# A 16-batch graph-attention kernel on one core: loads issued in half-size or quarter-size pieces, and batch 0's self features by seven block products

## The chip, the core and the metric

The kernel runs on one core of a Trainium2 chip. A core has five engines that run side by side, each with its own queue of instructions in program order: TensorE (PE, matrix products into PSUM), VectorE (DVE), ScalarE (ACT), GpSimd (POOL), and SyncE (SP), which here only issues transfers (DMAs). The metric is the device time of one launch in microseconds (us); the median of several runs is compared.

## The reference

For each of 16 batches there are N = 512 nodes with F = 512 features, one condition vector of 512, and an adjacency with 11 labels (here filled with zeros). The first NG = 20 nodes are the neighbours.

```
self_feat = concat(x, q or 0) @ W_self.T + b_self           # q only where a row of x sums to non-zero
output = self_feat
for d in 2 directions:
    kv = self_feat[:, :20];  qh = self_feat @ Wq[d].T + bq;  kh = kv @ Wk[d].T + bk     # 16 heads of 32
    aff = qh . kh / sqrt(32), masked where the labels' sum is 0, plus (labels @ w_bias + b_bias)
    output += (softmax(aff) @ kv) @ Wout[d] + bout
return x + relu(output)
```

## The kernel before

Everything is held transposed: features on the 128 partitions (four chunks c of 128), nodes in the free dimension. The kernel has a **setup** and a **loop** over batches b = 0 to 15, each with four tiles nt of 128 nodes.

**Setup** (lines 453 to 759). After the weights are loaded, `keys` (line 660) makes, in 22 bursts of eight matmuls, the keys already multiplied by Wq for all batches. A burst fills two PSUM buffers (`ps_g`), ACT empties one (line 684), DVE the other (line 686), into a staging tile `st`; from there SP stores them in DRAM, `g1_d` for batch 1 (line 694) and `g_d` for batches 2 to 15 (line 695). Both buffers are filled again by the next burst, so PE does other work between two bursts. The list `plan` (line 714) says which: `v` and `w` are parts of the value products (`values`, line 636, whose results POOL sends to DRAM as `vw_d`), `c` bias scores, `n` row flags, `b` biases, and `s` is a quarter of a block of batch 0's self features (`self_feat`, line 191, the plain product of x and W_self, finished by `self_copy`, line 210, on DVE). Three of the four blocks of batch 0 are made so in the setup; the fourth is made in the loop, in tile 1 of batch 0 (line 864).

**Self features of later batches** are made one batch ahead, in the loop, by seven products of half blocks instead of eight (a Winograd-Strassen scheme): `x_sum` (line 235) makes four sums of blocks of x on POOL, `weight_sums` (line 220) four of W_self once, `product` (line 246) runs the seven products in the order 1, 2, 6, 7, 5, 4, 3 into four PSUM banks (`ps_a` twice, `ps_d`, `ps_c`), and DVE adds them up in `partial` (line 281, on the accumulating `ps_a`) and `joined` (line 294). `partial` puts its first three results into tiles `u` of their own, from which `joined` reads.

**A tile of the loop**: `scores` (line 346, 128 matmul records in the profile) multiplies self features with the keys `gs[b]`; `weigh` (line 364, DVE) adds `full` (mask and bias, made by `full_add` on POOL, line 336), takes the maximum and subtracts it; `expo` is on ACT; `normal` (line 404) sums on DVE and multiplies on POOL; `turn` (line 410) transposes on DVE. In tile 2, `attend` (line 417) multiplies the previous batch's weights with its values `vds`, then come additions (`finish`), ReLU and the residual (POOL), and `store` (line 447).

**Order of the transfers.** All loads and stores of the loop are issued by SP in program order. `behind` (line 95) makes a load wait for a named instruction of another engine (`done["exp"]` and the like), so that the loads come at chosen places; whatever stands behind a waiting load on SP waits too. A batch loads x (1 MB, two loads), `adj` (twice 440 KB), `xn` (x in the other layout, for the row sums; twice 512 KB), the keys (twice 608 KB), `cq` (four of 20 KB), the row flags `nz` (256 KB, which `row_mask`, line 168, wrote to DRAM as `nz_d`, 2 KB, before) and the values `vd` (four of 32 KB, `load_values`, line 132), and stores four chunks of 256 KB.

**The start of the loop.** The keys of batch 1 are loaded ahead of the loop (line 770). In tile 1 of batch 0 SP issues the adjacency of batch 1, `cq`, one transfer of 2 MB that clears `bd_d` (`clear_blocks`, line 140), and the first `xn`. In tile 2 `blocks` (line 147) rearranges the values of all batches from `vw_d` into `bd_d`, by 12 transfers from DRAM to DRAM with rows of 128 bytes.

## Time and profile before

| what | value |
|---|---|
| median of 3 runs | 593.66 us (593.51 to 594.92) |
| the profiled execution: its own time | 593.27 us |
| the profiled execution: span from the first to the last instruction | 591.5 us (so 1.77 us lie around it) |
| TensorE clock granted, mean | 0.995 |
| PE busy | 578.7 us (98%) |
| DVE, ACT, POOL busy | 492.3, 395.6, 384.2 us |
| setup, up to the first scores | 92.5 us |
| one batch in the loop, the shortest | 30.47 us |

The page of the profile lists busy times, a picture of the span in 40 slices, the DMA queues, and the chain of work that ended last. A row of the chain has start, duration, engine, tile written, line and number of records. A row of the timeline has start, duration, engine, line, operation, tile written and tiles read; in brackets stands how long the engine was idle before it and what ended that. `issue` there means that the profile shows nothing that the engine waited for. PEld is TensorE's loading of weights. A product of the seven is 32 matmul records, and each matmul record has one record of a weight load.

### The profile page before, as it was taken

How to read it: one execution, taken by the hardware profiler on the slowest of the kernel's cores; microseconds unless marked ns; L12 is line 12 of the kernel's file. 1: busy time of each engine (PE TensorE's matmuls, PEld its weight loads, DVE VectorE, ACT ScalarE, POOL GpSimd, SP SyncE). 2: the span in 40 equal slices, each digit the busy share in tenths (PEclk: the TensorE clock that was granted, in tenths of full speed). 3: DMA queues.
4: the chain of work that ended last, by engine and by line, in shares of the span. 5: the costliest groups of instructions: out<-in, count | busy, mean ns of one | idle time of the engine just before them, and what ended most of it. 6: DMA issues, size and time to landing. Idle time of an engine off the chain costs nothing.

```text
span 591.5 us, 30038 instructions
## 1 busy us (share of the span) xinstructions
PE 578.7 (98%) x13180; PEld 439.7 (74%) x13180; DVE 492.3 (83%) x785; ACT 395.6 (67%) x1162; POOL 384.2 (65%) x351
## 2 busy tenths in 40 slices
PE   8999999999999999999999999999999999999994
PEld 6654547888978687787878787788787878787882
DVE  0495565889898888999999999888989898989896
ACT  1234644587877677768686868677787877777661
POOL 2315663638677675758686777675858677776774
PEclk9999999999999999999999999999999999999997
DMA  8998999857848485767676766757585748582503
GB/s 294 385 406 299 332 376 329 257 126 199 223 154 229 155 236 148 206 168 209 184 208 163 223 173 202 171 181 208 164 217 170 216 149 232 158 238 85 167 13 142
DMA packets 98129, 124.10 MB, mean 210 GB/s; under 512 B 19952, under 2 KB 70160, under 8 KB 95952
## 3 DMA queue, kind: packets, MB, share of 16 engines
q1 hardware_dynamic: 96752, 120.31, 67.1%
q8 instruction: 103, 1.69, 1.2%
q0 software_dynamic: 672, 1.36, 1.0%
q10 hardware_dynamic: 576, 0.53, 0.3%
q14 instruction: 26, 0.21, 0.1%
HBM read 82.30 MB, written 40.24 MB: 207 GB/s over the span
## 4 chain that ended last, share of the span: by engine, by line
PE 94%; DVE 3%; DMA 1%; issue 1%; ACT 0%; POOL 0%; SPq 0%; DVEq 0%; POOLq 0%; ACTq 0%
PE ps_s L353 44%; PE ps_a L279 17%; PE ps_c L279 8%; PE ps_o L426 6%; PE ps_d L279 4%; PE ps_v L644 3%; PE ps_k L581 3%; PE ps_sf L202 2%; DMA ws_q<-in_wsT 1%; PE ps_kv L532 1%; DVE o L435 0%; PE ps_nz L186 0%; DVE wt L415 0%; DVE ps_s L371 0%; DVE sm L406 0%
## 5 line engine op out<-in xcount | busy, mean ns | idle before, releaser
L353 PEld LDWEIGHTS ps_s<-g,sf 128*32 128x32 f32 x8192 | 264.0, 110 | 19.8 <-issue 12.2
L353 PE MATMUL ps_s<-g,sf 128*32 128x152 f32 x8192 | 277.3, 293 | 0.5 <-ACT st L684 0.5
L334 ACT COPY both<-add 32x80 f32<-32x80 f32 x512 | 130.9, 256 | 54.8 <-DVE add L325 49.0
L408 POOL TENSOR_TENSOR s<-s,sm 128x640 f32<-128x640 f32 x63 | 80.3, 1275 | 98.0 <-DVE sm L407 98.0
L341 POOL TENSOR_TENSOR full<-cq,both 128x640 f32<-128x640 f32 x64 | 100.1, 1565 | 30.3 <-issue 24.3
L314 ACT ACTIVATE prod<-adj,wb_sb 128x80 f32<-128x80 int32 x330 | 112.5, 432 | 0.0
L380 ACT ACTIVATE s<-s 128x640 f32<-128x640 f32 x63 | 46.5, 738 | 69.4 <-DVE s L375 69.0
L444 POOL TENSOR_TENSOR o<-o,x 128x512 f32<-128x512 f32 x60 | 75.9, 1285 | 0.0
L367 DVE TENSOR_TENSOR full<-ps_s,full 128x608 f32<-128x608 f32 x63 | 49.1, 779 | 32.1 <-PE ps_s L353 26.6
L406 DVE TENSOR_REDUCE sm<-s 128x32 f32<-128x640 f32 x63 | 50.9, 808 | 8.8 <-ACT s L380 8.6
L279 PE MATMUL ps_a<-t,ws_s 128*32 128x246 f32 x960 | 55.5, 370 | 0.0
L371 DVE TENSOR_REDUCE ps_s<-full 128x32 f32<-128x640 f32 x63 | 52.2, 828 | 2.2
L415 DVE STREAM_TRANSPOSE wt<-s 128x640 f32<-128x640 f32 x63 | 52.8, 839 | 0.1
L375 DVE TENSOR_TENSOR s<-full,ps_s 128x640 f32<-128x640 f32 x63 | 51.6, 818 | 1.1
L426 PE MATMUL ps_o<-wt,vd 32*32 32x512 f32 (+5 forms) x816 | 40.8, 581 | 3.7 <-DVE wt L400 2.0
L279 PEld LDWEIGHTS ps_a<-t,ws_s 128*32 128x32 f32 x960 | 32.2, 110 | 15.5
L325 DVE TENSOR_REDUCE add<-prod 128x80 f32<-128x960 f32 x32 | 36.8, 1150 | 6.3 <-ACT prod L314 4.4
L244 POOL TENSOR_TENSOR t<-x 128x492 f32<-128x492 f32 x30 | 34.4, 1148 | 10.1 <-DVE full L367 5.2
L439 ACT ACTIVATE o<-o,bo 128x512 f32<-128x512 f32 x60 | 38.2, 708 | 0.6 <-POOL biased L881 0.6
L435 DVE TENSOR_TENSOR o<-ps_o,sf 128x512 f32<-128x512 f32 x60 | 36.8, 672 | 1.0 <-PE ps_o L426 1.0
L286 DVE SCALAR_TENSOR_TENSOR u<-nz,qw,ps_a 128x246 f32<-128x246 f32 x90 | 36.6, 449 | 0.0
L244 POOL TENSOR_TENSOR t<-x,t 128x492 f32<-128x492 f32 x30 | 34.4, 1147 | 1.2
(238 smaller groups left out, 722.7 us busy)
## 6 DMA issues: line engine op xcount, KB each, us to landing
g_d<-st SPq DMA_DIRECT2D x16, 1064.0 KB, 5.9
g<-g_d SPq DMA_DIRECT2D x28, 608.0 KB, 5.2
out_T<-o SPq DMA_DIRECT2D x60, 256.0 KB, 4.7
xn<-in_xn SPq DMA_DIRECT2D x28, 512.0 KB, 3.6
x<-in_xT SPq DMA_DIRECT2D x28, 512.0 KB, 4.3
adj<-in_adj SPq DMA_DIRECT2D x32, 440.0 KB, 5.0
nz<-nz_d SPq DMA_DIRECT2D x14, 256.0 KB, 4.0
wk<-in_wkT SPq DMA_DIRECT2D x2, 1024.0 KB, 8.0
```

The lines of the kernel that those rows point to most:

```text
L244: nc.gpsimd.tensor_sub(t, one, two)
L279: nc.tensor.matmul(to, lhs, x[:, k], start=start, stop=stop, skip_group_check=n != 2)
L314: nc.scalar.activation(p[:, :, l], a[:, :, l], AF.Identity, scale=wb_sb[:, l : l + 1])
L334: nc.scalar.copy(adds[b, h][bass.ts(a, R), :, g], add[r].rearrange("p (t m) -> p t m", t=2))
L341: nc.gpsimd.tensor_add(f, cqs[b].unsqueeze(1).to_broadcast(shape), adds[b, nt // 2][:, nt % 2].unsqueeze(2).to_broadcast(shape),)
L353: nc.tensor.matmul(bank[bass.ts(a, R), bass.ts(j, WD // HL)], sfs[b][:, k, bass.ds(nt * P + (2 * g + j) * R, R)], keys[:, k, a], start=(k ...
L371: nc.vector.tensor_reduce(mx, f, AX.X, ALU.max)
L375: nc.vector.tensor_sub(s, f, mx.unsqueeze(3).to_broadcast(full))
L408: done["normal"] = nc.gpsimd.tensor_mul(s, s, sm.unsqueeze(3).to_broadcast(full))
L415: nc.vector.transpose(wts[b][:, nt], s.rearrange("p a h m -> p (a h m)"))
L426: nc.tensor.matmul(banks[a][bass.ds(at // 2 * DH, n * DH)].rearrange("p (t n) -> p t n", n=32), vd[r, bass.ds(at * DH, n * DH)], wt[r, :, ...
L444: nc.gpsimd.tensor_add(o[:, c], o[:, c], xs[b][:, c])
```

## The change

It has two parts.

1. **Batch 0's self features** are made wholly in the setup, by the seven products (step `p` in `plan`), each followed at once by its `partial` or `joined`. The values, flags and bias scores move to earlier bursts; the seven products are the fillers of the last seven bursts that have one. `row_sums(1)` and `weight_sums` move from bursts 11 and 13 to burst 9, and four `x_sum` for batch 0 are added on POOL in burst 11. The fourth block in tile 1 of batch 0 goes. `partial` now always writes into the self features' own tile, where `joined` adds to it (the tiles `u` go), and `new_self` (ACT) is called ahead of the first `partial`.
2. **The loop's loads** are split: x into four pieces of 256 KB, `xn` and the keys into four of 256 and 304 KB, `adj` into four of 220 KB, each behind an instruction of its own, in the order in which these come. Two pieces of x move ahead into tile 3 of the batch before. Each stored chunk is issued as soon as its residual is added. `load_values(b - 1)` moves from tile 3 of batch b - 1 to tile 0 of batch b. In batch 0 the clearing of `bd_d` becomes four transfers of 512 KB, `xn` four pieces, and `blocks` comes later, in tile 2 behind a sum; the second adjacency half of batch 1 and the keys of batch 1 are issued behind `blocks`.

On **PE**, in the setup, around the bursts of fc = 2, hg = 2 and 3 (a row is: line, operation, tile written, tiles read, size, how many alike). Before:

```order
L644 MATMUL ps_v_650<-wo_sb,kvT 128x512 x2
L669 MATMUL ps_g(2, 2, 1, 0, 2)0_688<-khD,wq_sb 128x304 x2
L669 MATMUL ps_g(2, 2, 1, 0, 2)1_689<-khD,wq_sb 128x304 x2
L202 MATMUL ps_sf_10_706<-x_161,ws_v 32x236 x16
L669 MATMUL ps_g(2, 3, 0, 1, 2)0_727<-khD,wq_sb 128x152 x2
L669 MATMUL ps_g(2, 3, 0, 1, 2)1_728<-khD,wq_sb 128x152 x2
L202 MATMUL ps_sf_10_706<-x_161,ws_v 32x236 x16
```

And in the changed kernel, at the same bursts:

```order
L189 MATMUL ps_nz<-rx_553,ones 128x512
L644 MATMUL ps_g(2, 2, 1, 0, 2)0_678<-khD,wq_sb 128x304 x2
L644 MATMUL ps_g(2, 2, 1, 0, 2)1_679<-khD,wq_sb 128x304 x2
L259 MATMUL ps_a_0_696<-x_161,ws_v 32x246 x8
L259 MATMUL ps_a_1_697<-x_161,ws_v 32x246 x8
L644 MATMUL ps_g(2, 3, 0, 1, 2)0_720<-khD,wq_sb 128x152 x2
L644 MATMUL ps_g(2, 3, 0, 1, 2)1_721<-khD,wq_sb 128x152 x2
L259 MATMUL ps_d_737<-x_161,ws_v 32x246 x16
```

Half a plain block (16 matmuls) between two bursts has become a whole product of the seven (16 matmuls too); the value products that stood around it are earlier.

On **SP**, from the last store of the setup to the first loads for batch 2 (`g_943` and `g_1193` are the keys of batch 1, `adj_1` the second half of its adjacency). Before:

```order
L695 DMA g_d<-st_885 128x2128
L130 DMA g_943<-g_d 128x16x152
L114 DMA adj_0_1038<-in_adj 128x2x440
L119 DMA cq_1040<-cq_d 32x160 x4
L142 DMA bd_d<-zero 128x16x256
L114 DMA adj_1_1046<-in_adj 128x2x440
L109 DMA xn_0_1048<-in_xn 128x1024
L109 DMA xn_1_1050<-in_xn 128x1024
L159 DMA bd_d<-vw_d 64x20x32
```

Changed, down to the first transfer of `blocks`:

```order
L670 DMA g_d<-st_913 128x2128
L117 DMA adj_0_1063<-in_adj 128x2x440
L145 DMA bd_d<-zero 128x4x256 x2
L122 DMA cq_1067<-cq_d 32x160 x4
L145 DMA bd_d<-zero 128x4x256 x2
L111 DMA xn_0_1152<-in_xn 128x512 x2
L111 DMA xn_1_1159<-in_xn 128x512 x2
L162 DMA bd_d<-vw_d 64x20x32
```

Changed, from the last two transfers of `blocks` on:

```order
L162 DMA bd_d<-vw_d 64x12x32
L162 DMA bd_d<-vw_d 64x20x32
L117 DMA adj_1_1191<-in_adj 128x2x440
L133 DMA g_1193<-g_d 128x4x152 x4
L105 DMA x_1467<-in_xT 128x512 x4
```

The keys of batch 1 have moved from the head of this piece to behind all twelve transfers of `blocks`, and so has the second half of its adjacency.

On **SP**, in batch 1, from the loads of x to the first keys. Before:

```order
L105 DMA x_1548<-in_xT 128x2x512 x2
L171 DMA nz_d<-nz_2_1583 128x4
L114 DMA adj_0_1609<-in_adj 128x2x440
L175 DMA nz_1639<-nz_d 128x512
L119 DMA cq_1641<-cq_d 32x160 x4
L114 DMA adj_1_1650<-in_adj 128x2x440
L109 DMA xn_0_1779<-in_xn 128x1024
L109 DMA xn_1_1781<-in_xn 128x1024
L130 DMA g_1895<-g_d 128x8x152
```

Changed:

```order
L105 DMA x_1467<-in_xT 128x512 x4
L174 DMA nz_d<-nz_2_1577 128x4
L139 DMA vd_1600<-bd_d 32x256 x4
L117 DMA adj_0_1608<-in_adj 128x440 x2
L178 DMA nz_1639<-nz_d 128x512
L122 DMA cq_1641<-cq_d 32x160 x4
L117 DMA adj_1_1650<-in_adj 128x440 x2
L111 DMA xn_0_1728<-in_xn 128x512 x2
L111 DMA xn_1_1783<-in_xn 128x512 x2
L133 DMA g_1790<-g_d 128x4x152 x2
```

Each load is split into two (x into four), and the values `vd` now stand between the write of the flags and the adjacency.

The diff, cut to its core (in the order of the code):

```diff
-    def load_xn(b, h, ins=None):
-        t = xns[b, h] = load.tile([P, 2, F], F32, tag="xn", name=f"xn{b}_{h}")
-        behind(nc.sync.dma_start(t, xn[b].rearrange("(p j) f -> p j f", j=4)[:, 2 * h : 2 * h + 2]), ins)
-
-    def load_adj(b, h, ins=None):
-        t = adjs[b, h] = load.tile([P, 2, S * L], I32, tag="adj", name=f"adj{b}_{h}", bufs=3)
+    def load_xn(b, h, ins=None, js=slice(0, 2)):
+        if js.start == 0:
+            xns[b, h] = load.tile([P, 2, F], F32, tag="xn", name=f"xn{b}_{h}")
+        rows = xn[b].rearrange("(p h j) f -> p h j f", h=2, j=2)[:, h]
+        behind(nc.sync.dma_start(xns[b, h][:, js], rows[:, js]), ins)
...
-    def clear_blocks(zero):
-
-        nc.sync.dma_start(
-            bd_d.rearrange("c b r e i g -> (c b r) (e i g)").rearrange("(n p) w -> p n w", p=P),
-            zero.unsqueeze(1).to_broadcast([P, C * B * 32 // P, HL * 2 * DH]),
-        )
+            ), ins if c == 0 else None)
+
+    def clear_blocks(zero, c, ins):
+
+        behind(nc.sync.dma_start(
+            bd_d[c].rearrange("b r e i g -> (b r) (e i g)").rearrange("(n p) w -> p n w", p=P),
+            zero.unsqueeze(1).to_broadcast([P, B * 32 // P, HL * 2 * DH]),
+        ), ins)
...
     def x_sum(b, n):
 
-        t = sums[b, n] = xsum.tile([P, 2, HN], F32, tag=f"t{n}", name=f"t{b}_{n}")
+        if b > 0:
+            t = xsum.tile([P, 2, HN], F32, tag=f"t{n}", name=f"t{b}_{n}")
+        else:
+            if n == 1:
+                held[0] = sfp.tile([P, C, N], F32, tag="sf", name="t0")
+            t = held[0][:, n - 1, : 2 * HN].rearrange("p (k n) -> p k n", k=2)
+        sums[b, n] = t
         one, two = {
             1: lambda: (x_block(b, 0, 1), x_block(b, 0, 0)),
             2: lambda: (x_block(b, 1, 1), sums[b, 1]),
             3: lambda: (x_block(b, 1, 1), x_block(b, 0, 1)),
             4: lambda: (x_block(b, 1, 0), sums[b, 2]),
         }[n]()
-        nc.gpsimd.tensor_sub(t, one, two)
+        done["xsum"] = nc.gpsimd.tensor_sub(t, one, two)
...
-    def partial(b, n, f, l, to=None):
-
-        if to is None:
-            to = us[b, n] = xsum.tile([P, 2, HN], F32, tag=f"u{n}", name=f"u{b}_{n}")
+    def partial(b, f, l):
+
+        to = block(b, f, l)
...
-    def joined(b, n, key, f, l):
-
-        nc.vector.tensor_add(
-            block(b, f, l), parts[b, key][:, : 2 * HN].rearrange("p (i n) -> p i n", i=2), us.pop((b, n))
+    def joined(b, key, f, l):
+
+        done["joined"] = nc.vector.tensor_add(
+            block(b, f, l), parts[b, key][:, : 2 * HN].rearrange("p (i n) -> p i n", i=2), block(b, f, l)
...
-            def self_step(b, f, h, i, k):
-                self_feat(b, f, h, ((i, (k,)),))
-                if (i, k) == (1, C - 1):
-                    self_copy(b, f, h)
+            def block_product(n):
+
+                product(0, n)
+                f, args = {
+                    1: (partial, (0, 0, 0)), 2: (joined, (0, "d", 0, 0)), 6: (partial, (0, 0, 1)),
+                    7: (partial, (0, 1, 1)), 5: (joined, (0, "c", 1, 1)), 4: (partial, (0, 1, 0)),
+                    3: (joined, (0, "c", 0, 1)),
+                }[n]
+                f(*args)
...
+                "p": [(block_product, (n,)) for n in (1, 2, 6, 7, 5, 4, 3)],
                 "v": [(values, (t, (d,), k)) for t in range(2) for d in range(2) for k in range(C)],
                 "w": [(values, (2, (0, 1), k)) for k in range(C)],
             }
-            plan = "bvv vv vv ccw vv ns ssss sssw vv vv ssss ssss vv vv nww ssss ssss".split()
+            plan = "bvv vvc vvc vvn vv vvw vv vv ww wn p p p p p p p".split()
...
+                if n == 9:
+                    row_sums(1)
+                    weight_sums()
                 if n == 11:
-                    row_sums(1)
-                if n == 13:
-                    weight_sums()
+                    new_self(0)
+                    for i in range(1, 5):
+                        x_sum(0, i)
...
-        load_keys(1)
...
-                    load_adj(1, 1)
-                    load_xn(2, 0)
-                    load_xn(2, 1)
-                if b == 0 and nt == 2:
-                    blocks()
-                if nt == 2 and last or nt == 3 and b == 0:
+                if nt == 2 and last:
...
-                            load_x(b + 1, range(2), done["exp"])
-                            load_x(b + 1, range(2, C), done["partial"])
+                            load_x(b + 1, range(2, 3), done["sum"])
+                            load_x(b + 1, range(3, C), done["normal"])
                         for g in range(2):
                             scores(b, nt, g, ps[g], range(2, C))
                         if more:
                             row_mask(b + 1)
                         mask_count(b, 1)
-                        joined(b, 3, "c", 1, 1)
+                        joined(b, "c", 1, 1)
                         product(b, 3)
+                        load_values(b - 1, done["joined"])
                         mask_sum(b, 1)
                         if more:
-                            load_adj(b + 1, 0, done["masks"])
+                            load_adj(b + 1, 0, done["masks"], slice(0, 1))
                     mask_spread(b, 1, (0, 1))
                     if last:
                         biased = work.tile([P, C, N], F32, tag="o", name="biased")
@@ -847,25 +822,26 @@
                     full_add(b, 1)
                     if more:
                         x_sum(b + 1, 1)
+                        if b > 0:
+                            load_adj(b + 1, 0, done["xsum"], slice(1, 2))
...
-                        load_nz(b + 1, done["exp"])
-                        load_cq(b + 1)
+                        load_nz(b + 1, done["weigh"])
+                        load_cq(b + 1, done["exp"])
                     normal(*prev)
+                    if b == 0:
+                        clear_blocks(zero, 2, done["sum"])
+                        clear_blocks(zero, 3, done["normal"])
                     if b > 0 and more:
-                        load_adj(b + 1, 1, done["normal"])
-                    if b == 0:
-                        self_feat(0, 1, 1)
+                        load_adj(b + 1, 1, done["normal"], slice(0, 1))
                     for g in range(2):
                         scores(b, nt, g, ps[g])
-                    if b == 0:
-                        self_copy(0, 1, 1)
...
+                            load_adj(b + 1, 1, done["xsum"], slice(1, 2))
+                        else:
+                            load_xn(2, 0, done["xsum"], slice(0, 1))
                         x_sum(b + 1, 3)
+                        if 0 < b < B - 2:
+                            load_xn(b + 2, 0, done["xsum"], slice(0, 1))
+                        elif b == 0:
+                            load_xn(2, 0, done["xsum"], slice(1, 2))
                     full_add(b, 2)
+                    if b == 0:
+                        load_xn(2, 1, done["full"], slice(0, 1))
...
-                            load_xn(b + 2, 0, done["add"])
-                            load_xn(b + 2, 1, done["relu"])
+                            load_xn(b + 2, 0, done["add", 1], slice(1, 2))
+                            load_xn(b + 2, 1, done["add", 3], slice(0, 1))
                     normal(*prev)
+                    if b + 2 < B:
+                        load_xn(b + 2, 1, done["sum"], slice(1, 2))
+                    if b == 0:
+                        blocks()
+                        load_adj(1, 1)
+                    if more:
+                        load_keys(b + 1, range(1), done["normal"])
                     for g in range(2):
                         scores(b, nt, g, ps[g])
                     if more:
                         product(b + 1, 1)
                         product(b + 1, 2)
-                    s = weigh(b, nt, pair, (lambda: partial(b + 1, 1, 0, 0)) if more else None)
+                        new_self(b + 1)
+                    s = weigh(b, nt, pair, (lambda: partial(b + 1, 0, 0)) if more else None)
                     expo(s)
                     turn(*prev)
-                    if b > 0 and more:
-                        load_keys(b + 1, range(2), done["exp"])
                     if more:
                         full_add(b, NT - 1)
+                        load_keys(b + 1, range(1, 2), done["full"])
                     if b > 0:
                         for c in (0, 1):
                             residual(b - 1, c, o)
+                            store()
...
+                    joined(b + 1, "d", 0, 0)
                     x_sum(b + 1, 4)
+                    load_keys(b + 1, range(2, 3), done["xsum"])
...
-                    partial(b + 1, 2, 0, 1)
+                    partial(b + 1, 0, 1)
                     mask_sum(b + 1, 0)
-                    if b > 0:
-                        load_keys(b + 1, range(2, C), done["masks"])
+                    load_keys(b + 1, range(3, C), done["normal"])
...
-                        residual(b - 1, 2, o)
-                        store()
-                        load_values(b)
-                        residual(b - 1, 3, o)
+                        for c in (2, 3):
+                            residual(b - 1, c, o)
+                            store()
+                    if b + 2 < B:
+                        load_x(b + 2, range(1), done["weigh"])
+                        load_x(b + 2, range(1, 2), done["exp"])
                     full_add(b + 1, 0)
```

80 lines of the change are left out of this document (25 added, 55 removed).

## The prediction

> **What bounds the kernel now.** I read the page first, then the windows of single stretches, then the chain of waits, and last the transfers around one stall. On the page I look at the busy times, the chain by engine and the queue of instructions.
>
> ```profile
> PE 578.7 (98%) x13180; PEld 439.7 (74%) x13180; DVE 492.3 (83%) x785; ACT 395.6 (67%) x1162; POOL 384.2 (65%) x351
> q8 instruction: 103, 1.69, 1.2%
> PE 94%; DVE 3%; DMA 1%; issue 1%; ACT 0%; POOL 0%; SPq 0%; DVEq 0%; POOLq 0%; ACTq 0%
> ```
>
> PE carries 94% of the chain, so only two things can pay: less work for PE, or fewer of the holes in it. The 1% "issue" is such a hole: PE waits for nothing that the program names. The 103 packets of queue 8 hold 1.69 MB, 16,384 bytes each. They are instructions: 13180 matmuls and as many weight loads, 26360 in all, are 256 to a packet.
>
> The windows give the span, then busy time and count of PE, PEld, DVE, ACT, POOL, then granted clock, DMA share and GB/s. The first is the end of the setup, the others are batches, from one tile 2 to the next; the last takes thirteen batches together.
>
> ```profile
> 59.00:92.00 33.00, 33.00 (x388) 16.40 (x384) 19.59 (x34) 16.16 (x39) 21.01 (x22) 1.00 0.96 354
> 135.77:166.72 30.95, 30.95 (x788) 26.61 (x792) 28.27 (x45) 23.67 (x71) 23.31 (x21) 1.00 0.76 205
> 166.72:198.55 31.83, 31.44 (x788) 24.27 (x792) 28.79 (x45) 24.29 (x73) 23.06 (x21) 1.00 0.66 194
> 198.55:230.66 32.11, 31.65 (x789) 24.46 (x792) 28.12 (x43) 23.75 (x73) 22.26 (x20) 1.00 0.65 184
> 261.14:291.62 30.48, 30.48 (x788) 24.15 (x792) 27.83 (x44) 23.53 (x71) 21.87 (x20) 1.00 0.67 191
> 352.77:384.77 32.00, 31.45 (x789) 24.34 (x792) 29.04 (x45) 24.48 (x73) 23.37 (x21) 1.00 0.69 190
> 384.77:415.92 31.15, 31.15 (x789) 24.32 (x792) 27.57 (x43) 22.65 (x71) 21.27 (x19) 1.00 0.67 190
> 135.77:538.00 402.23, 400.83 (x10196) 317.93 (x10200) 363.14 (x560) 305.87 (x923) 287.08 (x249) 1.00 0.68 191
> ```
>
> The setup has no hole in its last 33 us, at full clock. An undisturbed batch takes 30.48; thirteen of them would be 396.2, the loop takes 402.23, so **6.05 us** are lost. The five long rows have 0.47, 1.35, 1.63, 1.52 and 0.67 of it. The chain in the fourth of them shows the hole, in `attend`, and the page of transfers just ahead of it shows the load:
>
> ```profile
> 381.08 1.05 PE ps_o L426 x27
> 382.13 0.55 issue
> 382.68 2.10 PE ps_o L426 x21
> GB/s 239 223 398 334 445 382 368 398 121 66 48 33 58 96 27 55 14 27 41 14 0 0 14 14 14 0 123 123 123 55 41 123 123 178 287 396 424 383 287 232
> adj<-in_adj SPq DMA_DIRECT2D x1, 440.0 KB, 5.3
> q8 instruction: 1, 0.02, 5.2%
> ```
>
> The rate line covers 375.00 to 380.15 in 40 slices: after a rush the engines move mostly under 60 GB/s for about 2 us, then the 440 KB of `adj` rush through in some 1.2 us, and no packet of queue 8 is there. The one packet, last line, comes in the window 380.15 to 381.30, as the rush ends. PE runs dry about a microsecond later. So PE's next 256 instructions come late when their fetch falls behind a load's rush.
>
> **A, the setup.** The fourth block of batch 0 leaves the loop, and 3 blocks in the setup become seven products.
>
> ```profile
> 59.41 1.73 PE ps_sf L202 x32
> 86.82 1.86 PE ps_sf L202 x32
> 89.67 1.86 PE ps_sf L202 x32
> 96.86 3.45 PE ps_sf L202 x64
> 118.68 1.66 PE ps_a L279 x32
> ```
>
> Before there are six half blocks as fillers, four of 236 columns like the first row and two of 256 like the second and third: 4 x 1.73 + 2 x 1.86 = 10.64. A product of 246 columns took 1.66 in the loop. But 64 records of 256 columns took 3.45 there, 1.73 for 32, and 1.86 between bursts: being a filler costs 0.13. So a product as filler is 1.79 and seven are 12.5: **+1.9** (bounds: +1.0 at 1.66 each). I take 1.9, since the 1.86 row stands at the same place. The first scores move from 92.52 to 94.4.
>
> DVE has to empty a burst and sum a product in the time of one burst and one filler. The burst between the second and third row above lasts from 88.68 to 89.67, 0.99; with 1.79 that is 2.78:
>
> ```profile
> 86.91 1.17 DVE L686 TENSOR_SCALAR st<-ps_g(3, 2, 0, 1, 2)1_842 128x304 f32<-128x304 f32 x2 [0.34 <-PE ps_g(3, 2, 0, 1, 2)1_842 L669]
> 110.51 0.84 DVE L286 SCALAR_TENSOR_TENSOR u<-nz,qw,ps_a 128x246 f32<-128x246 f32 x2
> 103.01 1.14 POOL L244 TENSOR_TENSOR t<-x,t 128x492 f32<-128x492 f32 x1
> ```
>
> 1.17 + 0.84 = 2.01 against 2.78: hidden by PE's own work. POOL's four sums are 4.6 us, issued two bursts ahead of the products that need them, and POOL is busy for 21 of these 33 us: hidden. If that cover is gone, each late sum shows on PE one for one, at most about 1 us.
>
> **B and C, batch 0.** Here are PE's chain and the work on POOL and SP, where the clock of the batch starts at its first scores, T (92.52 before):
>
> ```profile
> 92.52 4.34 PE ps_s L353 x128
> 110.66 0.77 issue
> 123.67 4.13 PE ps_s L353 x128
> 105.31 1.56 POOL L341 TENSOR_TENSOR full<-cq,both 128x640 f32<-128x640 f32 x1
> 95.09 0.37 SPq L130 DMA_DIRECT2D g<-g_d  x1
> 104.61 1.96 SPq L109 DMA_DIRECT2D xn<-in_xn  x2
> 109.83 12.07 SPq L159 DMA_DIRECT2D bd_d<-vw_d  x12
> L159 SPq DMA_DIRECT2D bd_d<-vw_d x12: 611/716/1806, 109.8 to 121.2; - x12
> g<-g_d SPq DMA_DIRECT2D x28, 608.0 KB, 5.2
> ```
>
> The scores of batch 1 start at 123.67, T + 31.15. The block (3.45) goes, and with it perhaps the stall at 110.66 (some 0.98 with the slow start behind it): T + 26.7. DVE then comes to wait for POOL's `full` of tile 2, about 0.5: T + 27.2.
>
> But the keys of batch 1 are now **behind `blocks`** on SP. The last `xn` waits for `full` of tile 2, whose end is 105.31 + 1.56 = 106.87, T + 14.35; two issues bring `blocks` to T + 15.35, at 0.5 us each (one of the keys took 0.37, one `xn` of twice the size 0.98). Its twelve issues took 12.07, its median one 0.716, its shortest 0.611: 12 x 0.611 = 7.3 to 12.1. I take 12 x 0.86 = 10.3, the pace of the last seven:
>
> ```profile
> 115.89 6.01 SPq L159 DMA_DIRECT2D bd_d<-vw_d  x7
> g<-g_d SPq DMA_DIRECT2D x1, 1216.0 KB, 8.0
> DMA to landing us min/median/max: 3.4/4.4/4.9
> ```
>
> Then the second half of `adj` is issued (0.45, my estimate from the same two rows) and the keys, which land 5.2 us behind their issue by the median (8.0, the second row, while the engines were full; 3.4 at least, the landing of `blocks`' own, the third row). So the first quarter lands at T + 15.35 + 10.3 + 0.45 + 5.2 = T + 31.3; the next three are issued 0.45 apart and needed 1.03 apart. So PE, which could go on at T + 27.2, waits 4.1 us for the keys, and the block's gain is gone: **+0.15** (-3.95 at 7.3 and 3.4, where PE's floor holds; +4.7 at 12.07 and 8.0). With A that is **+2.05** up to the scores of batch 1 (-2.95 to +6.6). Queued behind this wait on PE is everything; on SP only loads of batch 2 stand behind, which have 20 us.
>
> **D, the loop.** PE, DVE, ACT and POOL do the same per batch. SP issues about 30 transfers instead of 20, each some 0.45 us: 14 of 30 us. Each load waits for an instruction that comes ahead of the next load's, so none holds up another for long, and I price the issuing at nothing; its cover is the 16 us in which SP has nothing to issue. What changes is the rush. Of `adj`, half stands behind the flags' write, 220 KB, and it waits for `masks`. If each stall shrinks by the 1.2 us of the rush, 0.47, 1.35, 1.63, 1.52 and 0.67 become 0, 0.15, 0.43, 0.32 and 0: 0.9. The fetches also slide (the setup's PE stream is shorter by 64 instructions), and may fall on other pieces: I add 0.6. So **1.5** of the 6.05 stay (bounds 0 and 5.55, since nothing in the trace shows the pieces): **-4.55**.
>
> [...]
>
> **Sum**, from the profiled execution's own 593.27: 593.27 + 1.9 + 0.15 - 6.05 + 1.5 = **590.8**. That execution is 0.39 under the median of 593.66, so my time may be as much low.
>
> **Rivals.**
>
> *The keys come in time and the holes close.* If `blocks` is issued at its shortest pace and the keys land fast, PE's floor counts: -3.95 + 1.9 = -2.05, and 5.55 of the loop's 6.05 go: 585.7. For it: `blocks` had the engines half idle at times in its 12 us; against it: only the minimum rows give it.
>
> *The change doesn't do what it says*: the holes don't come from the size of loads, but from the 2 us at under 60 GB/s behind the flags' small write, and that write stays. Then the loop gives 0.5 and the time is 593.27 + 2.05 - 0.5 = 594.8. For it: in the rate line the engines are slow long before the rush. [...]
>
> *Slower: the values come late.* `load_values` moves from tile 3 of a batch to tile 0 of the next, behind `joined`, two tiles ahead of `attend`:
>
> ```profile
> 281.83 0.66 DVE L296 TENSOR_TENSOR sf<-ps_c,u 128x492 f32<-128x492 f32 x1
> 289.38 2.24 PE L426 MATMUL ps_o<-wt,vd 32*32 32x512 f32 x48
> vd<-bd_d SPq DMA_DIRECT2D x64, 32.0 KB, 3.9
> ```
>
> `joined` ends at 282.49, four issues of some 0.4 us bring the last to 284.0, and `attend` starts at 289.38: 5.4 us are there, and the median landing is 3.9. From 5.4 on every tenth counts on PE, fourteen times. At 6.0 that is 0.6 x 14 = 8.4: 590.8 + 8.4 = 599.2. For it: the flags' write goes ahead; against it: 1.5 us of room.
>
> *Slow `blocks`*: +4.72 + 1.9 with 1.5 left in the loop: 593.27 + 6.62 - 4.55 = 595.3.
>
> **How the numbers follow.** Forecast 0.44 (its own range 588.4 to 592.8: nothing left in the loop and A at 1.0, or 3.5 left), keys in time 0.22, no effect 0.15, slow `blocks` 0.10, late values 0.09. The range from 585.5 to 595.5 holds all but the last and the tails. A measurement of this kernel can tell about 0.3%, 1.78 us, from no change: faster is under 591.88, slower over 595.44. Faster takes three quarters of the forecast and all of the first rival, 0.55; slower takes the late values and half of what ends near 595, 0.17; 0.28 are left for no difference.
>
> **What would show it.** First scores near 94.4, no `ps_sf` row, and seven `ps_a`, `ps_c`, `ps_d` rows near 1.79 in the setup: A. Scores of batch 1 at T + 31 with PE idle ahead of them and a DMA of `g` as releaser: C; no idle there: the first rival. Thirteen batches in 397.7 with rows of "issue" under 0.4 us: D; over 401: the second. Idle PE at `attend` released by `vd`: the third. The forecast is wrong most easily where the fetch falls on another transfer than I think, since its whole gain is in the holes.

## The result, and the profile after

The changed kernel took 594.46 us (median of 22 runs, 592.51 to 597.39), the kernel before 593.72 in the runs beside it (591.39 to 595.68). The ratio is **1.0008, interval 0.9994 to 1.0022**: no change that can be measured, where 590.8 was forecast. The profiled execution took 592.66 us, with a span of 590.8. It is 1.8 us under the median; what the median has beyond it no profile of these runs shows (e10 below, the same kernel on another chip, has a longer wait at the same place).

So a change that touches every load came out at nothing. The page shows where to look: PE has 4 us less to do (574.6 against 578.7), and yet PE's share of the chain is smaller.

```profile
PE 574.6 (97%) x13148; PEld 435.3 (74%) x13148; DVE 493.0 (83%) x788; ACT 395.0 (67%) x1162; POOL 388.6 (66%) x355
q8 instruction: 103, 1.69, 1.2%
PE 92%; DVE 4%; issue 1%; ACT 1%; DMA 1%; POOL 0%; DVEq 0%; POOLq 0%; ACTq 0%
```

Three windows cut the span at the same places in both kernels: from the fifth of the 22 bursts of `keys` (its second half; it is the first with a filler behind it) to the first scores (T), batch 0 up to the first scores behind its `attend`, and the thirteen batches after it. Before:

```profile
41.14:92.52 51.38, 50.85 (x532) 24.57 (x533) 31.07 (x58) 24.21 (x56) 29.73 (x34) 1.00 0.93 340
92.52:135.70 43.18, 42.41 (x1105) 35.83 (x1105) 33.26 (x51) 25.87 (x84) 20.78 (x21) 1.00 0.78 227
135.70:537.93 402.23, 400.83 (x10196) 317.94 (x10192) 363.14 (x560) 305.87 (x923) 287.08 (x249) 1.00 0.68 191
```

Changed:

```profile
40.35:92.70 52.35, 51.83 (x564) 24.95 (x564) 34.24 (x63) 24.21 (x56) 34.04 (x38) 1.00 0.93 335
92.70:140.84 48.14, 41.32 (x1041) 33.10 (x1041) 32.62 (x49) 25.91 (x84) 22.05 (x22) 0.96 0.80 219
140.84:537.14 396.30, 396.30 (x10196) 315.59 (x10192) 361.80 (x560) 305.26 (x923) 285.77 (x248) 1.00 0.67 193
```

The setup costs 0.97 more. The loop gives 5.93: its 396.30 us are those of thirteen undisturbed batches (396.2 by the prediction), so no hole is left in them. Lengths of batches tell this better than PE's idle time. Before, span less busy time is only 1.40 of the 6.05 us, since the ends of matmuls are modelled: in the hole that the prediction looked at, PE's row has 0.55 us of idle time and that of its weight loads 1.46, where the batch lost 1.52. Batch 0 takes all of it back: 48.14 against 43.18, although its PE executes 64 matmuls less. It is also the only stretch where the granted clock, third number from the right, is under 1.00. (0.97 + 4.96 - 5.93 is 0.00; the 0.6 us by which the two executions differ lie ahead of the first window and behind the last.)

The chain of waits in batch 0 of the changed kernel:

```profile
92.70 6.67 PE ps_s L332 x200
99.37 1.34 issue
100.71 4.34 PE ps_s L332 x128
105.05 1.34 issue
...
122.69 4.50 DMA g<-g_d
127.19 0.04 issue
127.23 5.39 PE ps_s L332 x120
```

And SP in it:

```profile
108.72 12.12 SPq L162 DMA_DIRECT2D bd_d<-vw_d  x12
120.88 0.72 SPq L117 DMA_DIRECT2D adj<-in_adj  x1
121.72 2.52 SPq L133 DMA_DIRECT2D g<-g_d  x4
```

PE at the scores of batch 1:

```profile
126.32 0.58 PE L332 MATMUL ps_s<-g,sf 128*32 128x152 f32 x8 [3.81 <-DMA g<-g_d]
127.23 5.39 PE L332 MATMUL ps_s<-g,sf 128*32 128x152 f32 x120 [0.33 <-DMA g<-g_d]
```

Two new holes stand in the first scores. Then PE waits for the keys of batch 1. Their first quarter, issued at 121.72 behind `blocks`, lands at 126.2; PE runs the eight score records that need no more (T + 33.6; before, these scores started at T + 31.15), waits again, and goes on at T + 34.5, when the second quarter has landed. The other 120 records then take 5.39 us, where 128 took 4.13.

### The profile page after: what moved, and what is told of

The parts are those of the page before. It is cut to its first block, busy times and chain, and to the rows that moved or that the text cites. A ratio compares the mean times of both kernels' runs of the same rounds, so it can differ in the third digit from the quotient of the medians.

```text
span 590.8 us, 30261 instructions
## 1 busy us (share of the span) xinstructions
PE 574.6 (97%) x13148; PEld 435.3 (74%) x13148; DVE 493.0 (83%) x788; ACT 395.0 (67%) x1162; POOL 388.6 (66%) x355
## 4 chain that ended last, share of the span: by engine, by line
PE 92%; DVE 4%; issue 1%; ACT 1%; DMA 1%; POOL 0%; DVEq 0%; POOLq 0%; ACTq 0%
PE ps_s L332 43%; PE ps_a L259 17%; PE ps_c L259 9%; PE ps_o L405 5%; PE ps_d L259 4%; PE ps_v L619 3%; PE ps_k L556 3%; PE ps_kv L507 2%; DMA g<-g_d 1%; ACT both L313 1%; PE ps_warm L466 1%; DVE wt L394 0%; DVE ps_s L350 0%; DVE o L414 0%; DVE full L346 0%
## 5 line engine op out<-in xcount | busy, mean ns | idle before, releaser
L313 ACT COPY both<-add 32x80 f32<-32x80 f32 x512 | 130.8, 256 | 57.2 <-DVE add L304 51.4
L259 PE MATMUL ps_a<-t,ws_s 128*32 128x246 f32 x1024 | 59.2, 371 | 0.0
L265 DVE SCALAR_TENSOR_TENSOR sf<-nz,qw,ps_a 128x246 f32<-128x246 f32 x128 | 51.6, 443 | 0.6 <-PE ps_a L259 0.6
L224 POOL TENSOR_TENSOR t<-x 128x492 f32<-128x492 f32 x32 | 36.8, 1150 | 8.6 <-DVE s L354 6.6
L405 PE MATMUL ps_o<-wt,vd 32*32 32x512 f32 (+5 forms) x816 | 37.0, 587 | 2.3 <-DVE wt L379 2.0
L224 POOL TENSOR_TENSOR t<-x,t 128x492 f32<-128x492 f32 x32 | 36.6, 1145 | 1.3
```

Of the source, the lines that this page charges most:

```text
L224: done["xsum"] = nc.gpsimd.tensor_sub(t, one, two)
L259: nc.tensor.matmul(to, lhs, x[:, k], start=start, stop=stop, skip_group_check=n != 2)
L265: done["partial"] = nc.vector.scalar_tensor_tensor(to[:, i], nzs[b][:, half(l)], qw[:, 2 * f + i, b : b + 1], parts[b, "a"][i][:, :HN], AL ...
L313: nc.scalar.copy(adds[b, h][bass.ts(a, R), :, g], add[r].rearrange("p (t m) -> p t m", t=2))
L405: nc.tensor.matmul(banks[a][bass.ds(at // 2 * DH, n * DH)].rearrange("p (t n) -> p t n", n=32), vd[r, bass.ds(at * DH, n * DH)], wt[r, :, ...
```

## The experiments

Beside each ratio (to the kernel before, measured with it on the same chip) stand the three stretches, cut in each profile as above; all in us.

| kernel | fifth burst to T | batch 0 | thirteen batches | ratio and interval |
|---|---|---|---|---|
| before | 51.4 | 43.2 | 402.2 | 1 |
| changed | 52.4 | 48.1 | 396.3 | 1.0008 (0.9994 to 1.0022) |
| e10, changed again | 52.4 | 48.9 | 396.2 | 1.0040 (1.0023 to 1.0057) |
| e1, keys ahead of `blocks` | 52.4 | 45.2 | 396.9 | 0.9995 (0.9976 to 1.0014) |
| e2, part 1 alone | 52.4 | 42.6 | 401.1 | 0.9995 (0.9978 to 1.0012) |
| e3, part 2 alone | 51.4 | 50.3 | 396.9 | 1.0028 (1.0012 to 1.0045) |
| e4, pieces in pairs | 52.4 | 50.3 | 396.2 | 1.0039 (1.0021 to 1.0057) |
| e5, keys ahead of the loop | 52.4 | 45.9 | 396.3 | 0.9995 (0.9980 to 1.0010) |
| e6, e5 with a small start | 52.4 | 50.7 | 396.2 | 1.0043 (1.0023 to 1.0063) |
| e7, before with halves | 51.4 | 42.8 | 397.4 | 0.9944 (0.9929 to 0.9960) |
| e8, both, batch 0's order of before | 52.4 | 43.4 | 396.2 | 0.9949 (0.9931 to 0.9967) |
| e9, e7 with part 1 and a small start | 52.4 | 41.3 | 400.7 | 0.9957 (0.9941 to 0.9972) |
| e11, the loop of part 2 alone | 51.4 | 43.4 | 397.0 | 0.9940 (0.9925 to 0.9956) |
| e12, `adj` alone in halves | 51.4 | 42.9 | 400.8 | 0.9990 (0.9974 to 1.0007) |

The times that were expected below were set against 593.7 for the kernel before; on the chips of these runs it took 591.0 to 591.5, so it is the stretches that decide. Their row for the kernel before comes from the one profile of it, taken beside the changed kernel where it took 2.2 to 2.7 us more, so a difference of about 1 us from that row says little: e2, whose loop has the loads of before, has 401.1. Ratios differ between chips too: the changed kernel has 1.0008 on one and 1.0040 on another (e10), so it is nowhere faster.

### Which part gives, and which takes: e2 and e3

e2 is the kernel before with part 1 (no split load); e3 is the changed kernel with `self_feat` and its plan put back, the fourth block in tile 1 of batch 0.

> The kernel before with part 1 alone: batch 0's self features by seven products in the setup, all loads as before. PE's instruction stream is the one of the changed kernel, so the fetches of its instructions fall at the same places. Theory K (the holes of the loop come from large loads): keys of batch 1 in time, batch 0 takes 40 to 42 us, and thirteen batches still take 401 to 403 us: 591 to 593. Rival (the holes went because the stream has slid by 64 instructions, not because of the loads): thirteen batches take 396 to 397 us and the time is 586 to 588.

> The changed kernel without part 1: the loads in pieces, but batch 0's self features as plain blocks, the fourth of them in tile 1 of batch 0 as before. PE's stream is the one of before. Theory K: thirteen batches take 396 to 397 us, since the pieces close the holes; the keys of batch 1 are as late as in the changed kernel, about T + 34.5, which the fourth block covers in part; 592 to 595. Rival (sliding of the stream): thirteen batches take 401 us or more, 597 to 600.

```profile
134.56:535.69 401.13, 399.52 (x10197) 318.77 (x10192) 362.47 (x560) 305.64 (x923) 288.33 (x250) 1.00 0.66 192
141.27:538.17 396.90, 396.90 (x10199) 314.84 (x10194) 361.95 (x560) 305.47 (x923) 286.11 (x248) 1.00 0.65 192
```

These are the thirteen batches of e2, then of e3. With PE's stream of the changed kernel and the loads of before the holes stay (401.13 us, and the span is 1.61 over PE's busy time); with the stream of before and the pieces they are gone. So the loads close them, and that the stream slides by 64 instructions does not. e2 (590.85 us) also shows what part 1 is worth alone: batch 0 gets 0.6 shorter, not 3.45, mainly because a new hole of 2.30 us stands in its first three tiles; the one of 0.77 us that stands behind them in the kernel before is still there, with 0.75.

### Size or spreading: e4, e7 and e12

e4, one of its pairs (the others likewise):

```diff
-                            load_adj(b + 1, 0, done["masks"], slice(0, 1))
+                            load_adj(b + 1, 0, done["masks"], slice(0, 1))
+                            load_adj(b + 1, 0, None, slice(1, 2))
...
-                        if b > 0:
-                            load_adj(b + 1, 0, done["xsum"], slice(1, 2))
```

> The changed kernel with one edit in the loop: the pieces keep their size, but the second of each two is issued right behind the first instead of behind an instruction of its own. Theory S (what counts is that the pieces are spread, so that the engines have no long backlog when a fetch comes): holes come back, thirteen batches take 398 to 402 us, 2 to 5 us more than the changed kernel. [...]

e7, on the kernel before, with the same for `xn`, x and keys:

```diff
-        behind(nc.sync.dma_start(t, a), ins)
+        for j in range(2):
+            behind(nc.sync.dma_start(t[:, j : j + 1], a[:, j : j + 1]), ins if j == 0 else None)
```

> The kernel before with one edit: each load of x, xn, adj and keys in the loop is issued as two transfers of half the size, back to back at the same place. Nothing is moved, nothing else is spread. Theory S (size alone makes the holes of the loop): thirteen batches take 396 to 397.5 us instead of 402, ratio 0.990 to 0.993. Rival (spreading, or the moved places): thirteen batches take 400 to 403 us, ratio 0.998 to 1.002.

e12 has only the lines shown, for `adj`.

> The kernel before with one edit: only the adjacency loads (440 KB) are issued as two halves back to back. Theory A (the holes stand behind the adjacency load that follows the flags' write, as the one hole that the prediction looked at): thirteen batches take 397 to 399 us, 3 to 5 us less than before. Rival (any large load that a fetch meets makes a hole): thirteen batches take 400 to 402 us.

The thirteen batches of e4, e7 and e12:

```profile
143.17:539.37 396.20, 396.20 (x10199) 314.78 (x10194) 361.76 (x560) 305.33 (x923) 286.19 (x248) 1.00 0.63 193
135.33:532.77 397.44, 397.44 (x10197) 315.06 (x10193) 362.15 (x560) 305.79 (x923) 287.41 (x249) 1.00 0.66 193
135.58:536.40 400.82, 400.44 (x10197) 319.88 (x10192) 362.87 (x560) 305.72 (x923) 286.70 (x249) 1.00 0.68 192
```

My theory of spreading fell. In e4 the second piece follows right behind the first, and not one hole comes back (what e4 loses against the changed kernel is in batch 0, and e10, the changed kernel again, loses as much). In e7 nothing is moved or spread at all: each load is two transfers instead of one, and 4.8 of the 6.05 us are gone by the two profiles; by the medians, measured on one chip, e7 is 3.0 us faster than the kernel before. What counted here is the size of one transfer. And it is no single load: halving `adj` alone, behind which the hole that the prediction looked at stood, gives 1.4 at most. That is little more than the 1.1 by which e2 lies below the kernel before without a split load, and the ratio (0.9990) shows no change.

### What batch 0 waits for: e1, e5 and e10

e1, in tile 2 of batch 0:

```diff
                     if b == 0:
-                        blocks()
                         load_adj(1, 1)
-                    if more:
+                        for c in range(C):
+                            load_keys(1, range(c, c + 1))
+                        blocks()
+                    elif more:
                         load_keys(b + 1, range(1), done["normal"])
```

> The changed kernel with one edit: in tile 2 of batch 0 the second adjacency half and the four pieces of keys of batch 1 are issued ahead of the 12 transfers of blocks instead of behind them. Theory K (the loop's holes are gone; batch 0 gives the gain back, because PE waits for these keys): the scores of batch 1 start near T + 30 instead of T + 34.5, no DMA of g as releaser, the granted clock stays at 1.00 in the 15 us behind it, and the time falls by 4 to 6 us against the changed kernel, to about 589. The two holes of 1.34 us in the first scores stay. Rival (the keys are only the last of several things that are late at that place): the scores start at T + 33 or later and the time falls by less than 2 us.

The keys no longer wait, and the clock stays at 1.00 (0.997 over the span). But `blocks` now issues from 113.89 to 127.66, and the chain shows who is late in their place:

```profile
127.02 6.01 DMA bd_d<-vw_d
133.03 0.02 SPq L139
133.05 0.04 issue
133.09 2.66 DMA vd<-bd_d
```

The values of batch 0 can be loaded only when the last of `blocks` has landed; `attend` waits for them for 1.1 us. Batch 0 falls from 48.1 to 45.2, three microseconds, less than the theory's 4 to 6 and more than the rival's 2. By the ratios it is 0.8 us against 1.0008 and 2.7 against e10's 1.0040.

e5 issues the keys where the kernel before does (`for c in range(C): load_keys(1, range(c, c + 1))` ahead of the loop, the later calls only for b > 0) and leaves `blocks` in its place.

> The changed kernel with the keys of batch 1 issued where the kernel before has them, ahead of the loop, in four pieces; blocks stays where the change put it. Theory K (SP issues the 12 transfers of blocks for 12 us, and either the keys behind them or, with the keys ahead of them, the values read from their result come late): with the keys off that queue, blocks starts at about T + 16 as in the changed kernel, the values land near T + 37, and neither the scores of batch 1 nor attend waits. Batch 0 takes 42 to 43.5 us instead of 48.1, with the two holes at its start left; ratio to the kernel before 0.992. Rival (the keys' 1.2 MB now stand ahead of PE's fetches at the start of batch 0): these holes grow by 2 us or more, and the ratio is 0.996 or above.

Batch 0 takes 45.9, not 42 to 43.5, and the holes at its start did not grow (1.61 and 0.79). DVE shows the third load that stands behind `blocks`:

```profile
126.77 1.07 DVE L298 TENSOR_REDUCE cond<-adj 128x80 f32<-128x880 int32 x1 [3.62 <-DMA adj<-in_adj]
127.76 0.66 DVE L275 TENSOR_TENSOR sf<-ps_c,sf 128x492 f32<-128x492 f32 x1
128.47 1.87 PE L259 MATMUL ps_c<-x,ws_s 128*32 128x246 f32 x32 [2.11 <-DVE sf L275]
```

The count of labels for batch 1 waits 3.62 us for the second adjacency half; behind it on DVE stands `joined`, and PE waits for that. So there are three, keys, adjacency and values, and the 12 us in which SP issues `blocks` make one of them late.

> The changed kernel again, for a second profile on this chip beside the two runs that undo its losses. Theory K: the scores of batch 1 wait 3 to 5 us for the keys, the two holes of 1.0 to 1.6 us stand in the first scores, batch 0 takes 47 to 51 us and thirteen batches 396 to 397. Rival (the profiled execution was a lucky one, and the median holds holes in the loop): thirteen batches take 398 us or more.

e10 confirms the place: no hole in the loop, and PE waits for the keys again, now for 5.81 us where it was 3.81; batch 0 takes 48.9. Only one hole, of 1.28 us, stands at its start, so PE comes to the wait earlier (T + 28.2, in the first profile T + 29.8), and the first quarter of the keys lands a little later (T + 33.9, there T + 33.5).

### The holes at the start: e6

On e5, the last store of the setup (1064 KB) is issued in four parts and `bd_d` is cleared by eight transfers of 256 KB:

```diff
-                        nc.sync.dma_start(g_d[C * fc + hg], st[:, 2:])
+                        cuts = (2, 6, 10, 13, B) if (fc, hg) == (C - 1, C - 1) else (2, B)
+                        for u, v in zip(cuts, cuts[1:]):
+                            nc.sync.dma_start(g_d[C * fc + hg, :, u - 2 : v - 2], st[:, u:v].rearrange("p b h d m -> p b (h d m)"))
```

> The run with the keys ahead, and the two transfers that stand ahead of the two fetches at the start of batch 0 made smaller: the last store of the setup (1064 KB) in four, the clearing of bd_d in eight transfers of 256 KB, each pair back to back. Theory S (a fetch waits for the transfer that an engine is in, so its size sets the hole): the two holes of 1.3 us shrink to 0.5 or less, and it is 1.5 to 2.5 us faster than the run with the keys ahead. Rival (a fetch waits for all that is queued): the holes stay at 1.1 to 1.6 us each, and the time is that of the run with the keys ahead.

PE in the changed kernel, then PE, DVE and SP in e6:

```profile
100.71 4.34 PE L332 MATMUL ps_s<-g,sf 128*32 128x152 f32 x128 [1.34 <-issue]
106.39 0.85 PE L332 MATMUL ps_s<-g,sf 128*32 128x152 f32 x20 [1.34 <-issue]
```

```profile
91.90 12.61 PE L333 MATMUL ps_s<-g,sf 128*32 128x152 f32 x384 [0.52 <-ACT st L660]
131.58 1.03 PE L260 MATMUL ps_c<-x,ws_s 128*32 128x246 f32 x5 [6.81 <-DVE sf L276]
129.88 1.07 DVE L299 TENSOR_REDUCE cond<-adj 128x80 f32<-128x880 int32 x1 [7.17 <-DMA adj<-in_adj]
110.44 12.81 SPq L163 DMA_DIRECT2D bd_d<-vw_d  x12
```

All 384 records of the first three tiles run without a hole (two of 0.59 and 0.62 us come behind them): size again, now of a store and a filling that the change left large (both were split at once, so which of them made which hole isn't told apart). But it is 0.4% slower than before, not faster. `blocks` is issued until T + 31.4 (in e5 T + 28.8), so the adjacency behind it lands at T + 38.0 (T + 34.6); PE gets to its wait earlier, at T + 32.9 (T + 34.2), waits 6.81 us there, and the granted clock stands at 0.50 for 10.2 us. Neither theory had that; closing holes ahead of a late arrival was worth nothing while the arrival stayed late.

### What is left of it: e8, e9 and e11

e8 puts batch 0's transfers back into the order of before (keys, `adj`, `cq`, clearing, second `adj`, `xn`, then `blocks`) in the small pieces of e6; all else is the changed kernel. e9 is e7 with part 1 and the same small start. e11 is the kernel before with only the loop's loads as changed.

> Both parts, but batch 0 issues its transfers in the order of the kernel before (keys of batch 1 ahead of the loop; in tile 1 adjacency, clearing, second adjacency half, xn; then blocks), all in small pieces back to back, the last store of the setup in four. The loop is the changed kernel's. Theory K with S (batch 0 lost its gain through what stands behind blocks on SP, and through holes at large transfers): nothing of batch 1 is behind blocks but the values, so batch 0 takes 39.5 to 41 us and thirteen batches 396.3: 4 to 6 us less than before, ratio 0.986 to 0.991. Rival (the row of blocks on SP only moves what is late, and now the values are): attend waits 1 to 3 us for them, batch 0 takes 43 us or more, ratio 0.994 or above.

> The kernel before with part 1, its loop loads halved back to back as in the run with halves alone, and batch 0's transfers in the same small pieces as its sister run; the places of the loads are those of before. Theory K with S: batch 0 takes 39.5 to 41 us instead of 42.8, thirteen batches 396.2 to 397.5, and the ratio is 0.986 to 0.991, about 2 to 3 us less than with halves alone (0.9944). Rival (part 1 gives nothing, since the plain block only covered fetches that now stop PE): batch 0 takes 42 us or more, ratio 0.993 or above.

> The kernel before with the changed kernel's loads in the loop alone: self features of batch 0 as plain blocks with the fourth in the loop, batch 0's transfers in the order and (but for xn, in halves) the sizes of before. Theory K (the whole of the change's gain is the loop's 6 us, and all else costs): batch 0 takes 42.5 to 43.5 us, thirteen batches 396 to 397, 5 to 6 us less than before, ratio 0.990 to 0.993. Rival (the values loaded two tiles ahead of attend, or other late loads, show once batch 0 is not late): thirteen batches take 398 us or more, ratio 0.995 or above.

By the profiles the loop gives its 5 to 6 us in e8 and e11, as the theory of e11 had it. By the medians on one chip e8 (588.48 us) is 3.0 us faster than the kernel before, e11 (587.52) 4.0 and e7 (588.01) 3.0. For e8 and e9 the theories failed, and the ratios are those of the rivals. Part 1 shows no gain in any of them. In e8 batch 0 takes 43.4, not 41: `xn` now lands late, at T + 24.0, ACT's copies behind it are late, and `attend` waits 0.7 us for the values. In e9 batch 0 is shortest, 41.3, but batch 1 takes 33.4, with PE waiting 2.5 us for DVE. e7, e8 and e11 can't be told apart by their intervals; e7 is the smallest edit, and e9 (0.9957) isn't ahead of them either.

## Why the prediction was wrong

**What bounds it, and D, right in kind and too small.** As I read the runs, the holes come from PE's instruction fetches meeting large loads: 29 of 32 end 1.26 to 1.61 us behind a packet of the instruction queue (last section), and with smaller loads they are closed (thirteen batches in 396.90 us in e3, 396.20 in e4, 397.44 in e7, where the kernel before takes 402.23). I left 1.5 of 6.05 us in the loop; 0.1 stay. My mechanism for the pieces was half right: they work by their size, not by their distance (e4, e7), and the adjacency load, whose rush I took 1.2 us off for, is at most one of several (e12).

The runs also tell two readings of a hole apart. e7 moved no load and gained 4.8 us from smaller transfers alone; in e4 the second piece stands right behind the first, so that as much is queued as with one whole load, and thirteen batches still take 396.20 us. Both speak against a fetch that waits for all that is queued. What a fetch does wait for, no run here shows.

**A, right for the products and too large by half for the stretch.** Seven products as fillers take 1.80 each, as predicted (1.79):

```profile
87.13 1.80 PE ps_a L259 x32
89.92 1.80 PE ps_c L259 x32
```

That is 12.60 us against 10.79 for the plain half blocks, +1.81 where +1.9 was forecast. But the stretch from the fifth burst to T grew by 0.97 (51.38 to 52.35, and by 0.98 in every run with part 1). What I missed is the rest of it. The six half blocks were not six whole fillers: one stood in pieces of 8 and 24 records (a letter `s` of the plan is 8 records, an eighth of a block of 64), and the bursts behind these two pieces took 1.4 us each where the others take 0.98:

```profile
57.48 0.54 PE ps_sf L202 x8
58.02 0.71 PE ps_g(1, 3, 1, 0, 2)0_552 L669 x4
```

The first of these bursts lasts from 58.02 to the half block at 59.41. In the changed kernel no burst takes more than 1.06. All bursts together take 0.78 less, the row flags 0.20 less, the bias scores 0.13 more: 1.81 - 0.78 - 0.20 + 0.13 is 0.96. Why the two bursts were slow the profile doesn't show.

**B, half wrong.** The stall at 110 went with the block, but two others came. PE's floor was right: in e8 and e9, where the keys are in time, the scores of batch 1 start at about T + 27.6 (T + 27.2 predicted). What I missed, as I read the rates, is that the plain block was also cover. Scores use up 256 instructions in 4.13 us, one 64-matmul block (128 instructions) in 3.45. Without it three tiles of scores stand back to back, and fetches whose packets started 3.2 to 4.0 us after PE began the 256 instructions before came with holes: 1.34 and 1.34 in the changed kernel, 2.30 in e2. With small transfers ahead of the fetches the same 384 records of e6 ran in 12.61 us without a hole.

**C, the step that failed.** The prediction's "+0.15" for the keys behind `blocks` was +3.38. `blocks` starts at T + 16.0 (15.35 predicted), issues for 12.12 us (10.3), and `adj` takes 0.84 until the keys' issue (0.45), so the keys are issued 2.9 us later than forecast. Their first quarter lands after 4.5 us (5.2), and its scores start at T + 33.6 instead of T + 31.3. But the first quarter isn't what PE needs: `scores` takes chunks 0 and 1 of the keys in turn, so PE wants the second quarter after eight records (0.3 us at the usual pace), not after 1.03 us. It lands 1.0 us behind the first, and the other scores go on at T + 34.5, on the path that sets the end. The waits for keys add up to 4.14 us, and 4.1 was forecast, but that is luck: the two holes kept PE busy until T + 29.8 (T + 27.2 predicted), and the keys were late by nearly as much. I had the row with 12.07 in hand and took the faster pace of its last seven; in the twelve further runs `blocks` took 10.95 to 13.77, in every order tried.

And the wait had an **after-effect** that no term covered: the granted clock.

```profile
123.50:126.00 2.50, 0.00 (x0) 0.00 (x0) 1.03 (x2) 0.66 (x3) 1.26 (x2) 1.00 1.08 347
126.00:128.50 2.50, 1.85 (x28) 1.18 (x32) 0.90 (x2) 2.50 (x9) 2.01 (x2) 0.61 1.15 341
128.50:131.00 2.50, 2.50 (x60) 2.13 (x56) 1.15 (x1) 0.83 (x4) 0.58 (x2) 0.71 1.07 388
126.54:129.96 3.42, 3.09 (x52) 2.18 (x48) 0.82 (x2) 2.50 (x8) 1.98 (x2) 0.50 1.11 363
```

Behind 3.81 us without a matmul the clock fell: 0.61 and 0.71 are means of 2.5 us, and the last row shows the 3.42 us in which it stood at 0.50. 120 records at the usual 4.13/128 are 3.87; they took 5.39, 1.52 more. With 3.38, less the 0.26 of the eight records that had run by then, that is 4.64 of the 4.96 that batch 0 lost. In e1 and e5, where PE waits 2.11 us at most in batch 0, the clock stayed at 1.00.

**The rivals.** The slow `blocks` (0.10) is nearest to what happened: 12.12, as it said. That its 595.3 lies near the 594.46 that came is luck. It took 8.0 us for the landing (4.5 came), 1.9 for A (0.97) and 1.5 for what is left in the loop (0.1), and it had neither the second quarter nor the clock. That the change does nothing in the loop is refuted by e3 and e4. Late values in every batch did not happen: PE has no wait for `vd` in the loop of the changed kernel. In batch 0 they are late only where `blocks` is issued later still (e1).

## What to carry to other kernels

Halve large transfers before you move them: back to back at the same place, that alone was worth 0.56% here (0.9944), and it needed no trigger and no new order. When a load is moved behind others on one issuing queue, add up the queue's own issue time from the longest row that the trace has of it, and ask of every load behind it, not only of the first, who waits, and which piece of it is needed first. And price a long wait on PE with its after-effect (a wait of 3.22 us was enough in e3: the clock stood at 0.50 for 6.8 us); work that leaves a stage may have been the cover of something else there.

## What the runs showed of the hardware

**From the first scores on, the clock fell at each of the five waits of PE of 3.22 to 6.81 us, and up to the end of batch 15 at none of 2.30 us or less.** e10 after a wait of 5.81 us:

```profile
122.70:125.20 2.50, 0.00 (x0) 0.00 (x0) 0.69 (x1) 0.61 (x2) 0.00 (x0) 0.73 1.10 357
125.20:127.70 2.50, 2.14 (x28) 1.39 (x32) 0.96 (x2) 2.50 (x9) 1.96 (x2) 0.50 1.15 331
127.70:130.20 2.50, 2.50 (x48) 1.95 (x40) 1.15 (x1) 0.84 (x3) 0.40 (x2) 0.50 1.08 392
```

e5 after 2.11 us:

```profile
125.70:128.20 2.50, 0.66 (x14) 0.33 (x4) 1.43 (x2) 1.43 (x5) 0.27 (x1) 1.00 0.82 287
128.20:130.70 2.50, 2.23 (x52) 1.61 (x56) 0.22 (x1) 2.31 (x7) 2.42 (x3) 1.00 0.20 43
```

The first 128 scores behind the wait in e10 took 7.03 us instead of 4.13. At waits of 3.22 (e3), 4.25 (e4) and 6.81 (e6) the clock stood at 0.50 too; behind 2.30 (e2) it stayed at 1.00. In e3 it fell inside the wait, 2.1 us after PE had stopped, and it stood at 0.50 for 3.42 us in the changed kernel, for 6.82 to 6.83 in e3, e4 and e10, and for 10.24 in e6: one, two and three times 3.41. But the length of a hole alone didn't decide it. A hole of 1.98 us stands at the end of every run. The 48 records behind it took 0.96 us in nine runs; in the changed kernel they took 1.44, at half the clock:

```profile
582.08:583.93 1.85, 0.00 (x1) 0.00 (x0) 1.75 (x4) 0.34 (x1) 1.81 (x2) 1.00 0.37 142
583.93:585.50 1.57, 1.44 (x48) 0.66 (x48) 0.98 (x3) 0.00 (x0) 0.39 (x1) 0.50 0.00 0
```

**Nearly every hole ended at about the same time behind a packet of instructions.** Over all runs there are 32 holes of more than 0.25 us marked "issue" from T to the last batch. In 29 of them PE went on 1.26 to 1.61 us after a packet of queue 8 had ended, and that packet had started 2.4 to 6.8 us after PE began the 256 instructions before the hole, as the trace counts them. The other three, one of about 0.6 us in each of e6, e8 and e9, ended 2.7 to 3.4 us after the last packet; what ended them isn't shown.
